# A decoder layer with a mixture of experts on one core: rows laid out by partition, expert biases moved, group tasks in halves

## The chip, the core and the metric

The kernel runs on one core of a Trainium2 chip. The metric is device time in microseconds (us) of one execution. A NeuronCore has TensorE (PE: matrix products into PSUM), VectorE (DVE), ScalarE (ACT), GpSimd (POOL) and SyncE (SP, which here only issues DMAs). Each runs its own list of instructions in order; they wait for each other on semaphores. PEld is PE's loading of weights.

## The reference, cut

```python
x = layernorm(x + attn(x, x, causal), ln1)              # 32 sequences of 128 tokens, D = 128
x = layernorm(x + attn(x, encoder, not causal), ln2)    # 16 heads of 8
# mixture of experts on the 4096 tokens
p = softmax(x @ rw + rb)                                # E = 8 experts
topw, topi = top_k(p, 2); topw = softmax(topw)
h = gelu(einsum('td,edf->etf', x, w1) + b1)             # FF = 512
eo = einsum('etf,efd->etd', h, w2) + b2
out = sum over the two chosen experts of topw * eo
x = layernorm(x + out, ln3)
```

All of it is float32. Only the two chosen experts of a token count.

## The kernel before, in words

**Units and halves.** A unit is one sequence of one attention: s (self, masked) or c (cross). Four sequences make a group (G = 4), so there are eight s groups and eight c groups. The units stand in one list: LEAD = 11 s units, then c and s in turn, then the c units that are left (lines 906 to 911). Each unit takes a slot of two halves. `half_slot(h)` (977) emits the work of one half: scores of the new unit and, with roles turned, of the unit two slots before (`both_scores`, 390), the row maximum on DVE (L425), exp on ACT (L433), for s a mask on POOL (L437); in even halves `values` (464) of the unit three slots before, in odd halves `outputs` (481). `ps_sc` and `ps_st`, where scores are put, have one buffer of PSUM each.

**Group tasks.** What is done once a group is put into a table of halves by hand (933 to 968), and `half_slot` runs what the table has for it. For an s group: `turn_input`, `keys`, `queries`, `values_of`, `residual`, later `turn_output`, `project` with `normalize` (304), `hand_over`. For a c group the same, and `keep_x2`, `route` (538), `place` (597) and `scatter` (678). Each task works on four sequences at once: a PSUM tile of 128x512, then one copy on ACT or one addition on DVE. `route` and `place` are generators of five steps, a step to a half. `scatter` issues two indirect DMAs on POOL to a half.

**The mixture.** `route` finds each token's two experts, `place` gives every (token, expert) pair a row in blocks of 128 rows of one expert, and `scatter` writes the token's row to DRAM (`xs`, 130 floats: the token, its row number, its first expert). There are two phases, PHASES: groups 0 to 5 and 6 to 7, with 55 and 23 blocks, 78 in all. When the last scatter of phase 0 has been issued, at half `start` (971), the blocks begin. `Pipeline.run` (851): for each block, SP fetches the weights of the block four ahead (`fetch_weights`, 745: 578 KB, w1, w2, b1 and a copy of b2 for every partition, into five buffers), PE does the first layer, ACT Gelu (L794), PE the second layer of the block before, DVE adds b2 from the weight tile (L810) into one of four `ot` buffers, POOL stores it by an indirect DMA to `eo` (L812). Every fourth block SP fetches 512 rows (`fetch_rows`, 733) and PE transposes them (`turn`, 759). After each block `beside` (1025) runs one more half of the table, and one step of each of up to two `combine`s (867). `combine` loads x2 and the two results of each token of a group (L872, L876), adds them with their weights, normalizes and stores (L901). The six groups of phase 0 begin theirs at the third block of phase 1, two at a time; the two of phase 1 after the last block.

**Queues.** SP issues all plain DMAs in the order of the program. A load that waits holds back everything after it on SP, weights too. The load of `gt` waits for all stores of its phase issued until then.

Of the kernel before, what the change touches and what calls it, by code (L numbers as in the profile page):

```python
# [24 lines left out]
PHASES = ((0, 6), (6, 2))  # L25
# [9 lines left out]
B2 = B1 + NFC  # L35
WP = B2 + P
# [5 lines left out]
LEAD = 11  # L42
# [19 lines left out]
def kernel(  # L62
# [140 lines left out]
    vs = [const.tile([P, G, H * VS + VC - VS - VW], F32, name=f"v_{i}") for i in range(3)]  # L203

    def blank(t):
        nc.gpsimd.memset(t, 0.0)
        nc.gpsimd.memset(
            t[:, :, : H * VS].rearrange("p b (h c) -> p b h c", c=VS)[:, :, :, HD:VW], 1.0
        )

    blank(vs[0])
# [41 lines left out]

    def load_router():
        nc.sync.dma_start(out=rw, in_=router_w)
        nc.sync.dma_start(
            out=rb, in_=router_b.rearrange("(o n) -> o n", o=1).broadcast_to([P, E])
        )
        nc.sync.dma_start(out=b1, in_=e_b1.rearrange("e (c f) -> (e c) f", f=P))

# [3 lines left out]
    blank_row = const.tile([P, XW], F32, name="blank_row")  # L264

    def routing_constants():
# [10 lines left out]

        i = setup.tile([P, B], I32, name="rowno_i")
        nc.gpsimd.iota(i, pattern=[[2 * P, B]], base=0, channel_multiplier=2)
        nc.vector.tensor_copy(rowno, i)  # L280
        later["free"] = counted([P, max(NBL)], [[2 * P, max(NBL)]], 0, "free")
        nc.gpsimd.memset(blank_row, 0.0)
        nc.gpsimd.memset(blank_row[:, TAG + 1 :], -1.0)
        nc.vector.tensor_copy(blank_row[:, TAG : TAG + 1], rowno[:, 0:1])
# [9 lines left out]
    x2d = tc.dram_tile([B, P, P], F32, name="x2d")  # L294
    xs = [tc.dram_tile([NBL[p] * P, XW], F32, name=f"xs_{p}") for p in range(NP)]
# [8 lines left out]
    def normalize(y, name):  # L304
# [3 lines left out]
        rs = small.tile([P, G], F32, tag="rs", name=f"rs_{name}")  # L308
        for t in range(G):
            nc.vector.bn_stats(st[:, t, :], y[:, t, :])  # L310
        for t in range(G):
            nc.vector.bn_aggr(mv[:, t, :], st[:, t, :])
        nc.gpsimd.tensor_scalar(rs, mv[:, :, 1], EPS, None, ALU.add)
        nc.gpsimd.tensor_tensor(rs, rs, mhalf, ALU.pow)
        yield
        for t in range(G):
            nc.vector.tensor_scalar(
                y[:, t, :], y[:, t, :], mv[:, t, 0:1], rs[:, t : t + 1], ALU.subtract, ALU.mult
            )

# [19 lines left out]
    def turned(src, name):  # L340
        pt = mm_tile([P, G, P], f"tp_{name}")
        for b in range(G):
            nc.tensor.transpose(pt[:, b, :], src[:, b, :], ident)
        return pt

    def turn_input(gr):
        pt = turned(gr.src, gr.name)
        gr.kvT = act.tile([P, G, P], F32, tag="kvT", name=f"kvT_{gr.name}", bufs=3)
        nc.scalar.copy(gr.kvT, pt)
        if gr.kind == "s":  # L350
            gr.qT = gr.kvT

    def keys(gr):
        pk = mm_tile([P, G, P], f"pk_{gr.name}")
        nc.tensor.matmul(pk, lhsT=gr.w.wk, rhs=gr.kvT, start=True, stop=True)
        gr.k = act.tile([P, G, P], F32, tag="k", name=f"k_{gr.name}", bufs=3)
        nc.scalar.activation(gr.k, pk, AF.Identity, bias=gr.w.bk)

    def queries(gr):

        pq = mm_tile([P, G, P], f"pq_{gr.name}")
        nc.tensor.matmul(pq, lhsT=gr.w.wq, rhs=gr.qT, start=True, stop=True)
        gr.qb = act.tile([P, G, 4, P], F32, tag="qb", name=f"qb_{gr.name}", bufs=3)
        for r in range(4):
            nc.scalar.activation(  # L365
                gr.qb[:, :, r, :], pq, AF.Identity,
                bias=gr.w.bqm[:, r : r + 1], scale=hmask[:, r : r + 1],
            )
# [4 lines left out]
    def values_of(gr):  # L373
        pv = mm_tile([P, G, P], f"pv_{gr.name}")
        for b in range(G):
            nc.tensor.matmul(pv[:, b, :], lhsT=gr.kvT[:, b, :], rhs=gr.w.wv, start=True, stop=True)
# [3 lines left out]
        nc.scalar.copy(  # L380
            gr.v[:, :, : H * VS].rearrange("p b (h c) -> p b h c", c=VS)[:, :, :, :HD],
            pv.rearrange("p b (h d) -> p b h d", d=HD),
        )
# [115 lines left out]
    def turn_output(gr):  # L499
        pt = turned(gr.o, f"o_{gr.name}")  # L500
        gr.oT = act.tile([P, G, P], F32, tag="oT", name=f"oT_{gr.name}")
        nc.scalar.copy(gr.oT, pt)

    def project(gr):

        py = mm_tile([P, G, P], f"py_{gr.name}")
        for b in range(G):
            nc.tensor.matmul(py[:, b, :], lhsT=gr.oT[:, b, :], rhs=gr.w.wo, start=True, stop=True)
        gr.y = act.tile([P, G, P], F32, tag="y", name=f"y_{gr.name}", bufs=3)
        nc.vector.tensor_tensor(gr.y, py, gr.resid, ALU.add)  # L510
        yield from normalize(gr.y, gr.name)

    def affineT(gr, i):

        pt = turned(gr.y, f"y_{gr.name}")
        t = act.tile([P, G, P], F32, tag=f"xT{i}", name=f"xT{i}_{gr.gi}")
        nc.scalar.activation(t, pt, AF.Identity, bias=lnbT[i], scale=lngT[i])
        return t

    def hand_over(gr, to):  # L520

        to.qT = affineT(gr, 0)
        to.resid = act.tile([P, G, P], F32, tag="x1", name=f"x1_{gr.gi}", bufs=4)
        nc.gpsimd.tensor_tensor(to.resid, gr.y, bc(lng[0], 1, G), ALU.mult)
        nc.gpsimd.tensor_tensor(to.resid, to.resid, bc(lnb1c, 1, G), ALU.add)

    def keep_x2(gr):
        gr.x2T = affineT(gr, 1)
        gr.x2 = act.tile([P, G, XW], F32, tag="x2", name=f"x2_{gr.gi}", bufs=3)
        x2 = gr.x2[:, :, :P]  # L530
        nc.gpsimd.tensor_tensor(x2, gr.y, bc(lng[1], 1, G), ALU.mult)
        nc.gpsimd.tensor_tensor(x2, x2, bc(lnb[1], 1, G), ALU.add)
        nc.gpsimd.tensor_copy(gr.x2[:, :, TAG], rowno[:, G * gr.gi : G * gr.gi + G])
        nc.sync.dma_start(
            out=x2d[G * gr.gi : G * gr.gi + G].rearrange("b p d -> p b d"), in_=x2
        )

    def route(gr):
# [25 lines left out]

        ex = small.tile([P, G], F32, tag="ex", name=f"ex_{gi}")
# [514 lines left out]
```

## Time and profile before

| | us |
|---|---|
| median of 3 runs (741.51 to 744.32) | 741.92 |
| the profiled execution, its time | 743.56 |
| its span, first to last instruction | 741.5 |
| PE busy, 8691 matmuls | 596.9 (80%) |
| PE weight loads | 486.4 (66%) |
| DVE busy | 421.4 (57%) |
| POOL busy | 364.7 (49%) |
| ACT busy | 347.8 (47%) |
| mean granted TensorE clock | 0.905 |
| moved by DMA | 88.06 MB |

Times in the profile are us unless marked ns. A row of the groups gives line, engine, operation, output and inputs, shapes and count, then busy time and the mean of one. The chain of work that ended last is followed back from the last instruction, at each step to what released it: here 43% PE, 17% DVE, 13% POOL, 13% DMA, 6% ACT. A row of the waits gives who waited for whom: total us, times, longest. Rows by stretch give the stretch, its length, and the busy us of each engine in it.

### The profile page before, as it was taken

What the parts mean: (1) busy time and instruction counts of PE and PEld (TensorE: products, weight loads), DVE (VectorE), ACT (ScalarE), POOL (GpSimd) and SP (SyncE); (2) the same over time, 40 slices, a digit from 0 to 9 for tenths busy, and PEclk for the clock granted to TensorE, in tenths of its full rate; (3) what the DMA queues carried; (4) which work ended last, traced back from release to release, by engine and by line L of the source; (5) the groups of instructions that cost most, each with busy time, mean ns of one, the idle gap of its engine ahead of it and who ended that gap; (6) DMA issues with size and microseconds to landing.
All of it is one profiled execution on the core that took longest, in us unless ns stands there. A gap on an engine that the chain in (4) does not pass through costs nothing.

```text
span 741.5 us, 21324 instructions
## 1 busy us (share of the span) xinstructions
PE 596.9 (80%) x8691; PEld 486.4 (66%) x8691; DVE 421.4 (57%) x1313; ACT 347.8 (47%) x671; POOL 364.7 (49%) x744
## 2 busy tenths in 40 slices
PE   5878898789898988888889878856887999875740
PEld 3556566667676766666667666746887999875630
DVE  2354665556776676687587587765522232274466
ACT  3335555465554556456455553533644555432310
POOL 2273555334447536645755633653776555433441
PEclk9798999999989999999999898976999999987975
DMA  6140603920100100100101100153998999979932
GB/s 135 26 98 3 152 22 78 187 35 4 44 2 27 49 2 24 52 2 17 45 3 31 31 2 10 38 179 113 314 309 283 354 355 344 331 252 307 280 122 89
DMA packets 73714, 88.06 MB, mean 119 GB/s; under 512 B 8080, under 2 KB 60336, under 8 KB 73616
## 3 DMA queue, kind: packets, MB, share of 16 engines
q1 hardware_dynamic: 68496, 77.19, 36.2%
q0 software_dynamic: 4544, 9.38, 3.5%
q8 instruction: 68, 1.11, 0.6%
q14 instruction: 30, 0.25, 0.1%
q10 hardware_dynamic: 576, 0.13, 0.1%
HBM read 67.90 MB, written 23.49 MB: 123 GB/s over the span
## 4 chain that ended last, share of the span: by engine, by line
PE 43%; DVE 17%; POOL 13%; DMA 13%; issue 6%; ACT 6%; SPq 1%; DVEq 0%; POOLq 0%
DMA wd<-wpk 7%; POOL xs L684 6%; PE st_s L410 5%; PE ph L789 5%; DVE m_c L425 5%; PE sc_s L397 4%; PE po L805 4%; PE po_s L472 4%; PE st_c L410 3%; DMA eo<-ot,to 3%; PE po_c L472 3%; ACT qb_s L365 3%; DVE m_s L425 2%; PE sc_s L417 2%; PE st_s L402 2%
## 5 line engine op out<-in xcount | busy, mean ns | idle before, releaser
L794 ACT ACTIVATE h<-ph,wd 128x128 f32<-128x128 f32 x312 | 88.8, 368 | 120.6 <-PE ph L789 84.1
L437 POOL TENSOR_SCALAR_AFFINE_SELECT pr_s<-pr_s 128x1024 f32<-128x1024 f32 x64 | 70.0, 1093 | 114.9 <-ACT pr_s L433 114.8
L789 PE MATMUL ph<-xT,wd 128*128 128x128 f32 x624 | 94.2, 298 | 39.6 <-DMA wd<-wpk 30.9
L812 POOL DMA_INDIRECT eo<-ot,to x78 | 77.1, 988 | 99.0 <-DVE ot L810 36.4
L425 DVE TENSOR_REDUCE m_s<-sc_s 128x8 f32<-128x1024 f32 x64 | 78.1, 1221 | 83.8 <-PE st_s L410 67.5
L789 PEld LDWEIGHTS ph<-xT,wd 128*128 128x128 f32 x624 | 83.2, 207 | 46.2 <-DMA wd<-wpk 33.4
L433 ACT ACTIVATE pr_s<-st_s 128x1024 f32<-128x1024 f32 x64 | 65.6, 1025 | 94.0 <-PE st_s L410 88.1
L425 DVE TENSOR_REDUCE m_c<-sc_c 128x8 f32<-128x1024 f32 x64 | 78.0, 1220 | 54.3 <-PE st_c L410 40.9
L433 ACT ACTIVATE pr_c<-st_c 128x1024 f32<-128x1024 f32 x64 | 65.5, 1024 | 63.2 <-PE st_c L410 59.4
L805 PE MATMUL po<-wd,h 128*128 128x128 f32 x624 | 89.1, 290 | 1.9 <-ACT h L794 1.9
L417 PE MATMUL sc_c<-k_c,qb_c 32*128 32x128 f32 x1024 | 78.4, 293 | 9.5 <-DVE m_s L425 5.0
L805 PEld LDWEIGHTS po<-wd,h 128*128 128x128 f32 x624 | 82.8, 206 | 2.1 <-ACT h L794 2.1
L417 PE MATMUL sc_s<-k_s,qb_s 32*128 32x128 f32 x1024 | 82.4, 303 | 0.2 <-ACT qb_s L365 0.2
L410 PE MATMUL st_c<-qb_c,k_c 32*128 32x128 f32 x1024 | 74.9, 282 | 0.0
L410 PEld LDWEIGHTS st_s<-qb_s,k_s 32*128 32x128 f32 x1024 | 73.1, 200 | 1.1 <-issue 1.1
L810 DVE TENSOR_TENSOR ot<-po,wd 128x128 f32<-128x128 f32 x78 | 22.3, 289 | 90.7 <-PE po L805 81.4
L417 PEld LDWEIGHTS sc_c<-k_c,qb_c 32*128 32x128 f32 x1024 | 65.7, 195 | 12.2 <-DVE m_c L425 6.3
L410 PE MATMUL st_s<-qb_s,k_s 32*128 32x128 f32 x1024 | 72.8, 283 | 0.9 <-issue 0.9
L410 PEld LDWEIGHTS st_c<-qb_c,k_c 32*128 32x128 f32 x1024 | 72.3, 195 | 0.5
L684 POOL DMA_INDIRECT xs<-x,slots x64 | 63.8, 997 | 15.7 <-issue 12.0
L417 PEld LDWEIGHTS sc_s<-k_s,qb_s 32*128 32x128 f32 x1024 | 68.8, 202 | 3.1 <-issue 2.1
L397 PE MATMUL sc_s<-causal,ident 128*128 128x512 bf16 x128 | 41.1, 405 | 24.7 <-DVE m_s L425 13.7
(226 smaller groups left out, 1070.4 us busy)
## 6 DMA issues: line engine op xcount, KB each, us to landing
wd<-wpk SPq DMA_DIRECT2D x78, 578.0 KB, 5.3
xt<-xs SPq DMA_DIRECT2D x18, 260.0 KB, 5.2
wpk<-in_L_xattn_e_w_dram SPq DMA_DIRECT2D x16, 256.0 KB, 6.9
gt<-eo SPq DMA_DIRECT2D x8, 512.0 KB, 6.3
xs<-blank_row SPq DMA_DIRECT2D x1, 3575.0 KB
xg<-in_x_dram SPq DMA_DIRECT2D x9, 256.0 KB, 3.3
eg<-in_ctx_dram SPq DMA_DIRECT2D x8, 256.0 KB, 3.5
x2d<-x SPq DMA_DIRECT2D x8, 256.0 KB, 2.5
```

The costliest lines, as they stand in the source:

```text
L397: nc.tensor.matmul(sc[:, i], lhsT=ident16, rhs=causal, start=True, stop=False)
L410: nc.tensor.matmul(st[:, i, r, :], lhsT=old.group.k[rowsof(g), old.b, :], rhs=old.group.qb[rowsof(g), old.b, r, :], start=False, stop=r == 3,)
L417: nc.tensor.matmul(sc[:, i, r, :], lhsT=new.group.qb[rowsof(g), new.b, r, :], rhs=new.group.k[rowsof(g), new.b, :], start=not new.masked, ...
L425: nc.vector.tensor_reduce(new.m[:, 8 * half : 8 * half + 8], sc.rearrange("p i r k -> p (i r) k"), AX.X, ALU.max,)
L433: nc.scalar.activation(old.pr[:, hs, :], st.rearrange("p i r k -> p (i r) k"), AF.Exp, scale=SCALE)
L437: nc.gpsimd.affine_select(out=old.pr[:, hs, :], in_=old.pr[:, hs, :], pattern=[[0, 8], [1, P]], compare_op=ALU.is_ge, fill=0.0, base=0, ch ...
L472: nc.tensor.matmul(po[VC * r : VC * r + VC, g, :], lhsT=u.group.v[:, u.b, at_v : at_v + VC], rhs=u.pr[:, h, :], start=e == 0, stop=e == 1,)
L684: i = nc.gpsimd.indirect_dma_start(out=xs[ph.p][:, :], out_offset=bass.IndirectOffsetOnAxis(ap=slots[:, k, t : t + 1], axis=0), in_=gr.x2[ ...
L789: nc.tensor.matmul(hid[:, c, :], lhsT=w[:, c * P : (c + 1) * P], rhs=self.xT[i // XB][:, i % XB, :], start=True, stop=True,)
L794: nc.scalar.activation(self.h[i][:, c, :], hid[:, c, :], AF.Gelu, bias=w[:, B1 + c : B1 + c + 1])
L805: nc.tensor.matmul(po, lhsT=h[:, c, :], rhs=w[:, W2 + c * P : W2 + (c + 1) * P], start=c == 0, stop=c == NFC - 1,)
L812: s = nc.gpsimd.indirect_dma_start(out=eo[p][:, :], out_offset=bass.IndirectOffsetOnAxis(ap=self.to[q][:, i % XB : i % XB + 1], axis=0), i ...
```

## The change

- `PHASES` becomes ((0, 5), (5, 3)): 47 and 31 blocks. `LEAD` becomes 12.
- DRAM by partition: `x2d` is [group, partition, sequence, 128], rows of `xs` that one partition reads lie together (four rows, 2080 bytes), and the two results of four tokens in `eo` too (4096 bytes). `place` computes the row numbers for it with integer steps; `rowno` follows.
- b2 leaves the weight tile (1028 floats a partition in place of 1156). `biases` multiplies the two chosen experts' weights into b2 by a matmul for a whole group, adds x2 and writes the sum to `x2d`, which `combine` starts from. The second layer's result is only copied to `ot`.
- `normalize` scales and shifts on ACT, with a bias of -mean * rs, in more steps. The weights of the two experts come from Tanh in place of Exp.
- Group tasks are done in two steps of two sequences; each step yields. `scatter` issues one DMA a step. Steps are put into halves by `book`, which takes, between two bounds, the half whose busiest engine would be least loaded by the planner's own costs.
- A group's `combine` begins as soon as its blocks are done (three blocks after the last that can hold its rows), not at the end of the phase; its `gt` takes a buffer of the tag "qb". Value tiles, `k` and `qb` have four buffers. The first fetch of rows is issued a half before the blocks, the first weights three.

The diff, cut to its core:

```diff
-PHASES = ((0, 6), (6, 2))
+PHASES = ((0, 5), (5, 3))
...
-B2 = B1 + NFC
-WP = B2 + P
+WP = B1 + NFC
...
-LEAD = 11
+LEAD = 12
...
@@ normalize
         for t in range(G):
-            nc.vector.tensor_scalar(
-                y[:, t, :], y[:, t, :], mv[:, t, 0:1], rs[:, t : t + 1], ALU.subtract, ALU.mult
-            )
+            nc.scalar.activation(
+                y[:, t, :], y[:, t, :], AF.Identity,
+                bias=rs[:, 1, t : t + 1], scale=rs[:, 0, t : t + 1],
+            )
+            if t == 1:
+                yield
...
+    PAIRS = (slice(0, 2), slice(2, 4))
...
     def keys(gr):
-        pk = mm_tile([P, G, P], f"pk_{gr.name}")
-        nc.tensor.matmul(pk, lhsT=gr.w.wk, rhs=gr.kvT, start=True, stop=True)
-        gr.k = act.tile([P, G, P], F32, tag="k", name=f"k_{gr.name}", bufs=3)
-        nc.scalar.activation(gr.k, pk, AF.Identity, bias=gr.w.bk)
+        gr.k = act.tile([P, G, P], F32, tag="k", name=f"k_{gr.name}", bufs=4)
+        for ab in PAIRS:
+            pk = pair(f"pk_{gr.name}", ab)
+            nc.tensor.matmul(pk, lhsT=gr.w.wk, rhs=gr.kvT[:, ab], start=True, stop=True)
+            nc.scalar.activation(gr.k[:, ab], pk, AF.Identity, bias=gr.w.bk)
+            yield
...
+    def biases(gr):
+        gi = gr.gi
+        w = small.tile([P, 2, G, E], F32, tag="comb", name=f"comb_{gi}", bufs=2)
+        for k in range(2):
+            nc.vector.tensor_tensor(
+                w[:, k], gr.onehot[:, k], bc(wts[:, k, G * gi : G * gi + G], 2, E), ALU.mult
+            )
+        nc.vector.tensor_tensor(w[:, 0], w[:, 0], w[:, 1], ALU.add)
+        yield
+        pw = mm_tile([G * E, P], f"pw_{gi}")
+        nc.tensor.transpose(pw, w[:, 0].rearrange("p b e -> p (b e)"), ident)
+        wT = small.tile([G * E, P], F32, tag="wT", name=f"wT_{gi}", bufs=2)
+        nc.scalar.copy(wT, pw)
+        yield
+        pb = mm_tile([P, G, P], f"pb_{gi}")
+        nc.tensor.matmul(pb, lhsT=wT, rhs=b2g, start=True, stop=True)
+        base = act.tile([P, G, P], F32, tag="base", name=f"base_{gi}", bufs=1)
+        nc.vector.tensor_tensor(base, pb, gr.x2[:, :, :P], ALU.add)
+        nc.sync.dma_start(out=x2d[gi], in_=base)
...
-        nc.scalar.activation(ex, ex, AF.Exp)
+        nc.scalar.activation(ex, ex, AF.Tanh, scale=0.5)
...
@@ second_layer
-            nc.vector.tensor_tensor(ot, po, w[:, B2:], ALU.add)
+            nc.vector.tensor_copy(ot, po)
...
+    def book(lo, hi, cost, *call):
+        def then(h):
+            old = busy.get(h, (0.0,) * 4)
+            return max(a + b for a, b in zip(old, cost) if b)
+        h = min(range(lo, max(lo, hi) + 1), key=lambda h: (then(h), h))
+        busy[h] = tuple(a + b for a, b in zip(busy.get(h, (0.0,) * 4), cost))
+        return at(h, *call)
+    def chain(lo, hi, *parts):
...
+        for n, (cost, call) in enumerate(todo):
+            left = len(todo) - 1 - n
+            end = book(lo, hi - left, cost, *call)
+            lo = end if hi - end + 1 >= left else end - 1
+            ends.append(end)
...
+        h, far = max(h, sent), 1 + (gi == NG - 1)
+        for b in range(G):
+            for k in range(2):
+                at(h, scatter, c, ph, b, k)
+                h += far
+        sent = h
+        if gi == PHASES[0][1] - 1:
+            ready = h
...
+    start = max(behind, ready)
+    at(start - 3, blocks.prepare)
+    at(start - 1, blocks.first_rows)
...
+        summed = {}
+        for p, (g0, n) in enumerate(PHASES):
+            for g in range(n):
+                i = NS + 2 * G * (g + 1) - 1 + 3
+                key = (p, i) if i < NBL[p] or p == NP - 1 else (p + 1, i - NBL[p])
+                summed[key] = groups["c", g0 + g]
```

## The prediction, as put on record

> **What bounds the kernel now.** I read the slices of the span first, then the busy time by stretches, then the chain and the waits.
>
> ```profile
> PE   5878898789898988888889878856887999875740
> ...
> PEclk9798999999989999999999898976999999987975
> DMA  6140603920100100100101100153998999979932
> ```
>
> Tenths of busy time, 18.5 us a slice. Attention fills slices 1 to 26 with PE at 0.8 to 0.9 and idle DMA. Then PE falls to 0.5 (the handover), the MoE blocks follow with PE and DMA both near 1.0, then both fall, and at the end PE is at 0.
>
> ```profile
> 317.00:375.00 58.00, 50.99 (x921) 38.69 (x920) 40.99 (x117) 31.40 (x44) 32.43 (x65) 0.94 0.07 20
> ...
> 480.00:507.00 27.00, 12.92 (x162) 10.76 (x160) 18.00 (x92) 6.63 (x10) 14.43 (x28) 0.71 0.45 148
> 507.00:540.00 33.00, 30.08 (x233) 29.18 (x232) 17.62 (x90) 20.25 (x57) 20.42 (x36) 0.87 0.74 244
> ...
> 580.00:640.00 60.00, 56.44 (x493) 55.12 (x493) 15.80 (x64) 33.13 (x116) 30.55 (x59) 1.00 1.01 349
> 640.00:690.00 50.00, 35.57 (x253) 34.31 (x253) 27.50 (x118) 16.91 (x60) 20.64 (x36) 0.83 0.90 283
> 690.00:715.00 25.00, 16.96 (x106) 16.15 (x105) 14.26 (x58) 7.04 (x25) 10.48 (x18) 0.80 0.64 204
> 715.00:742.00 27.00, 0.01 (x1) 0.00 (x0) 13.16 (x49) 0.00 (x0) 4.71 (x7) 0.60 0.36 105
> ```
>
> Stretch, length, then busy us of PE, PEld, DVE, ACT, POOL, then clock, DMA share, GB/s. A block is 17 PE instructions (8 + 8 + 1 transpose), so 580 to 640 holds 29 blocks at 2.07 us with PE at 94%: the good rate. 507 to 580 holds 29.5 at 2.5 us. 640 to 715, where six groups are combined, holds 21 at 3.6 us. The last 27 us have no PE work.
>
> Inside attention the reduce L425 shows the beat: where little stands beside it, starts are 2.49 us apart with a new cross unit (464.93, 467.42, 469.90 in DVE's timeline) and 3.19 us with a new self unit. Each score tile has one buffer, so scores wait for the reduce (1.22 us) before them. A steady period of 16 halves (8 units) took 58.4 us against 8 x 2.49 + 8 x 3.19 = 45.4 us of beat. PE is busy 51.3 us of it, so 7.1 us are all that better placing could return there.
>
> ```profile
> SPq L754 <- DVE ot L810: 35.5, 29, 3.2
> ```
>
> SP's own waits: 29 weight fetches waited for the DVE add that reads the bias out of the weight tile.
>
> **Part 1: attention.** A c and an s group bring some 15 us of PE work a period (rows L343, L355, L362, L376, L508, L545 divided by 8 groups), nearly all of the 13 us above the beat. Cutting it in twos removes none of it. It can fill halves in which PE waits: of those I count in one period a half of 5.5 us where POOL is busy 5.0 us (two scatters of 2 x 1.27 us, a mask, the rsqrt), one of 3.2 us with 1.5 us of PE behind DVE's normalize, and several of 0.5 to 1 us behind place, route and queries. One scatter to a half (0.99 + 0.09 + 0.2 us to issue) and booking remove most; I take idle 7.1 -> 3.
>
> Added: the bias step on PE, a transpose (0.2) and a 512-wide matmul (nearest row L362, 1.1): +1.3 us a period. On DVE three small steps (0.18 each) and an add of 512 (L510, 0.68), five integer steps in place (about 0.9). Normalize's 4 x 0.38 to 0.46 us move from DVE to ACT (nearest row: Gelu 128x128 with a bias pointer, 0.37 us). ACT also pays a fixed part for each extra half copy (586 ns for 512 wide, 372 for 256: 0.16 each, some 22 a period, 3.5 us). ACT goes from 31 to about 38 us of 58 and stays under PE. So a period changes by -4.1 + 1.3 = -2.8; 5.25 periods give **-15**. I worked the booking through on paper: where the window is shorter than the chain, the first parts collapse into one half (nine parts of s0 in half 15, of s7 in half 111, four parts of each c group). There PE waits for ACT's copy and DVE for POOL's rsqrt (1.04 us); I set these, some 6 us, against what the last 22 halves (78 us, beat 55) gain. The fourth value tile adds 1.3 us of POOL memsets (1.07 + 0.22) to half 9, which is 8.1 us long already for the routing constants; it is in those 6 us. The wider clearing of rows and the dropped bias copies cost and win nothing: DMA is 10% busy there (share 0.07 in the row above). Bounds: +8 (nothing recovered, all additions paid) and -30 (idle of the period to 0).
>
> A rule speaks against the move. The Trainium skill, "ScalarE: Activation LUTs", Rules for kernel authors, sends mul and add to VectorE. By its fixed costs a 128-wide ACTIVATE with two pointer operands is about 0.39 us back to back (an estimate); here DVE's own step took 0.36 to 0.46 us, so rule and row agree that nothing is won per instruction and only the busier engine matters.
>
> Exp becomes Tanh. The trace has six table loads of 1283 ns: one at the start, then none until the last group's two Exps and three for Gelu around them. If Tanh needed its own, 6 groups x 2 x 1.28 = 15 us of ACT would come into attention, mostly beside PE. That is the upper bound; 0 is the lower. I take 0 there, and 5 us of ACT in the first blocks (two groups now route there), hidden behind POOL. The same page, Table sets, lists Tanh with Exp in one set, which would make it 0 in attention; no run here shows it.
>
> **Part 2: handover.** With five groups in phase 0, its last scatter is booked at half 133, and the blocks start at 134 (before: 137). Now, from the last reduce to the first block:
>
> ```profile
> 476.06 1.23 DVE L425 TENSOR_REDUCE m_c<-sc_c 128x8 f32<-128x1024 f32 x1 [0.31 <-PE st_c L410]
> ...
> 499.72 1.08 PE L766 MATMUL px<-ident,xt 128*128 128x128 f32 x4 [4.34 <-DMA xt<-xs]
> ...
> 506.21 1.01 PE L789 MATMUL ph<-xT,wd 128*128 128x128 f32 x3 [5.40 <-DVE xT L781]
> ```
>
> That is 506.2 - 477.3 = 28.9 us. After: six halves of mostly POOL work (1.27 scatter, about 0.65 of other tasks each) 11.5, landing 2.7, rows 2.8 (both in the chain at 493.9 and 496.8), transposes 0.6, copy 0.7: 18.3. **-10**; bounds -17 (all but the DMAs hidden) and -2 (place of group 5 delays the copy on DVE as place of group 6 does now).
>
> **Part 3: the blocks.** Packets, from the trace's DMA records (medians): 512 B 27 ns, 1024 B 46, 2048 B 84, 4624 B 179, so about 8.4 ns + 0.037 ns a byte. Weights go from 4624 to 4112 B (160 ns; 128 x 19 / 16 = 0.15 us a block), rows xt from 4 x 28 to 85 ns (0.05 us a block), gt and x2d save 0.4 us a group. In all 78 x 0.2 + 3 = 19 us of the 191 us of DMA time from 507 to the end. And a weight buffer is freed by PE, not by DVE's add. A good block then is PE's 1.95 to 2.0 us.
>
> Against it: POOL. In blocks 0 to 18 it issues 19 stores of results and 16 scatters (groups 5, 6) at 1.27 us, plus 6.7 us of rsqrt and x2: 51 us, and only four ot buffers let PE run ahead. I take 48 us. Blocks 19 to 77: 59 x 2.0 = 118. Combines: the bursts of 640 to 715 cost 21 x (3.57 - 2.07) = 31 us for six groups, 5.3 each. Seven now come one by one, every eight blocks, with 1 MB each, but each gt load still waits on SP for the newest result to land (5.2 us median), with the next weights queued behind it. Between 1.3 (only the bytes) and 5.3 I take 4: 28. Sum 194 against 715 - 507 = 208: **-14**. Bounds -35 and +10.
>
> **Part 4: the end.** Two groups in step become one: stores landed, gt load, 8 x 0.35 of sums, statistics, rsqrt, 4 x 0.37 on ACT, two passes of 0.69, a store of 2.3 us: about 20.5 with the hand-offs, against 26.5. **-6**, bounds -9 and -2.
>
> **Sum.** 743.6 (the profiled execution; span 741.5) - 15 - 10 - 14 - 6 = 698.6. That execution lay 1.6 above the median of 741.9, so 697 against the runs; I say **698**.
>
> **Rivals.** A: everything overlaps. Attention -25, handover -14, blocks -32 (0 to 18 at 2.3 us, 1.5 a combine), end -7: 666. For it: the good rate of 580 to 640. Against: POOL's count above. B: placing gains nothing, PE sets every half and the bias step is paid: attention +5, rest as above: 718. For it: 51.3 of 58.4 us are already PE's. Against: the halves behind POOL. C, slower: SP's queue. The gt load's wait holds the weights, so blocks 19 to 77 run at the 3.36 us of 640 to 690: 59 x 1.36 = 80 in place of 28, +52: 750. It decides above about 11 us a combine (then 745). For it: that stretch itself. Against: there four groups came in 15 blocks, and pairs waited for the store of the pair before.
>
> **Chances.** Forecast (680 to 712) 0.56, A 0.18, B 0.16, C 0.10. The range reaches to A's and B's times and the bounds beside them: 668 to 734. A measurement here tells about 0.5% (3.7 us) from no change; of C's 0.10 a part ends near nothing: faster 0.87, same 0.04, slower 0.09.
>
> **What would show it.** Attention: last L425 reduce near 460 (before 476), PE share above 0.9 in the middle. Handover: 18 us from it to the first ph. Blocks: no "SPq L754 <- DVE ot", waits on POOL in the first 19, weights waiting behind gt at each combine. End: 20 us without PE. Table loads before the last scores would prove the Tanh step wrong; a middle period of 58 us or more Part 1; blocks over 2.6 us after the 19th Part 3.

## The result: no change that counts

The changed kernel took 741.48 us (median of 20 runs, 736.7 to 745.9), the kernel before 744.54 in the same series: ratio 0.9976, 95% interval 0.9952 to 1.0000. The forecast was 698. The profiled execution took 742.25 us, its span is 740.5, its mean granted clock 0.897 (before 0.905). PE is busy 606.3 us, DVE 413.0, ACT 404.6 (before 347.8), POOL 366.9; DMA moved 82.48 MB (before 88.06).

The slices of the span, to be laid beside those of the prediction:

```profile
PE   5696899999988999899889789868996786689750
...
PEclk9578999999999899899899999757999988899985
DMA  5010342630000100010110010052896788799852
```

Attention's PE row is a little fuller from slice 6 to 19. The start has a clock of 5 in the second slice, the handover (slices 26 to 28) one of 7, 5, 7, and the blocks no longer hold DMA at 9: it falls to 6 and 7 at regular places.

The trace gives the boundaries of the four terms of the prediction. "First block" is the start of the first ph.

| | before | after | forecast of the change | found |
|---|---|---|---|---|
| first reduce | 13.2 | 16.6 | | |
| start of the 23rd half's reduce | 100.1 | 109.1 | | |
| last reduce | 476.1 | 467.8 | -15 | -8.3 |
| its end to the first block | 28.9 | 31.3 | -10 | +2.4 |
| first block to PE's end | 208.8 | 214.0 | -14 | +5.2 |
| of it blocks 0 to 18 | 49.5 | 53.7 | | |
| PE's end to the end | 26.5 | 26.2 | -6 | -0.3 |

So three of four terms brought nothing or less, and the first, which went the right way, lost 9 us at its start. By stretch, in the columns of the prediction (a middle period; the handover; blocks 0 to 18, 19 to 46, 47 to 76; the end):

```profile
291.10:349.10 58.00, 51.87 (x939) 39.97 (x935) 42.51 (x121) 36.82 (x72) 32.72 (x67) 0.94 0.06 20
468.90:500.30 31.40, 22.08 (x200) 16.00 (x200) 11.13 (x66) 9.71 (x18) 12.66 (x28) 0.60 0.35 125
500.30:554.00 53.70, 48.08 (x373) 45.24 (x374) 33.85 (x174) 30.90 (x95) 34.85 (x62) 0.92 0.67 221
554.00:641.90 87.90, 61.60 (x480) 58.29 (x478) 35.29 (x152) 36.66 (x126) 48.29 (x90) 0.89 0.80 271
641.90:711.50 69.60, 62.54 (x507) 61.89 (x508) 27.20 (x113) 38.10 (x131) 34.88 (x64) 0.92 0.88 306
714.30:740.50 26.20, 0.05 (x1) 0.00 (x0) 10.11 (x41) 3.29 (x8) 7.69 (x13) 0.56 0.28 84
```

The fourth row is the surprise: 28 blocks, 3.14 us each, PE idle for 26 of 88 us. Most intervals between blocks there are 1.8 to 2.9 us (4.4 after block 19). After blocks 22, 30, 38 and 46 (counted from 0) they are 5.8, 8.8, 8.6 and 8.7, with 3.2 to 3.6 for the next. Each lies four blocks behind the one at which a combine issues its loads (18, 26, 34, 42). In the second row PE has work for 22 of 31 us, at a clock of 0.60 (before 14.8 us at 0.75).

**One combine, in the timeline** (start, length, engine, line; in brackets the idle time before and what ended it):

```profile
628.25 0.58 SPq L940 DMA_DIRECT2D acc<-x2d  x1
...
634.62 0.32 SPq L942 DMA_DIRECT2D gt<-eo  x1
...
635.04 0.38 SPq L816 DMA_DIRECT2D wd<-wpk  x1
...
638.11 1.14 DVE L955 SCALAR_TENSOR_TENSOR acc<-gt,wts,acc 128x128 f32<-128x128 f32 x4 [6.52 <-DMA gt<-eo]
...
638.79 1.03 POOL L878 DMA_INDIRECT eo<-ot,to  x1 [9.79 <-DVE acc L955]
...
641.16 0.68 DVE L847 COPY xT<-px 128x512 f32<-128x512 f32 x1
...
641.94 2.04 PE L855 MATMUL ph<-xT,wd 128*128 128x128 f32 x8 [6.22 <-DVE xT L847]
```

SP stands 6 us at gt, until the newest store of a result has landed, with the weights behind it (635.04). The stores after it wait on POOL, 9.79 us, because they write into the tensor that gt reads. DVE waits in order for gt, with the copy of the next four blocks' rows (L847) behind it. PE runs dry, and its next block runs at half clock (2.04 for eight matmuls; 1.06 before).

**The waits**, those of the whole span that bear on this (total us, times, longest):

```profile
POOL eo L878 <- DVE acc L955: 48.4, 11, 9.8
DVE acc L955 <- DMA gt<-eo: 46.0, 8, 7.4
...
PE ph L855 <- DMA wd<-wpk: 21.6, 8, 6.4
PE ph L855 <- DVE xT L847: 12.5, 5, 6.2
...
PE py_c L542 <- ACT oT_c L533: 9.7, 8, 2.2
```

and SP's own:

```profile
SPq L942 <- DMA eo<-ot,to: 44.5, 15, 6.5
SPq L820 <- PE po L871: 38.3, 35, 4.1
```

The second of SP's rows is as forecast: a weight buffer is freed by PE, no longer by DVE's add. The first is the new wait.

### The profile page after: what moved, and what is told of

Read it like the earlier page. It is cut to its first block, busy times and chain, and to the rows that moved or that the text cites. A ratio compares the mean times of both kernels' runs of the same rounds, so it can differ in the third digit from the quotient of the medians.

```text
span 740.5 us, 21783 instructions
## 1 busy us (share of the span) xinstructions
PE 606.3 (82%) x8779; PEld 499.5 (67%) x8779; DVE 413.0 (56%) x1321; ACT 404.6 (55%) x919; POOL 366.9 (50%) x747
## 2 busy tenths in 40 slices
DMA packets 48038, 82.48 MB, mean 111 GB/s; under 512 B 7968, under 2 KB 26464, under 8 KB 47936
## 5 line engine op out<-in xcount | busy, mean ns | idle before, releaser
L855 PE MATMUL ph<-xT,wd 128*128 128x128 f32 x624 | 92.2, 295 | 34.1 <-DMA wd<-wpk 21.6
L464 ACT ACTIVATE pr_s<-st_s 128x1024 f32<-128x1024 f32 x64 | 65.8, 1029 | 79.0 <-PE st_s L441 78.7
L448 PE MATMUL sc_c<-k_c,qb_c 32*128 32x128 f32 x1024 | 79.1, 295 | 10.7 <-DVE m_s L456 9.0
L448 PE MATMUL sc_s<-k_s,qb_s 32*128 32x128 f32 x1024 | 80.7, 300 | 0.0
L441 PE MATMUL st_c<-qb_c,k_c 32*128 32x128 f32 x1024 | 76.8, 290 | 0.0
L441 PEld LDWEIGHTS st_c<-qb_c,k_c 32*128 32x128 f32 x1024 | 75.8, 205 | 0.7
L876 DVE COPY ot<-po 128x128 f32<-128x128 f32 x78 | 22.5, 288 | 59.6 <-PE po L871 48.9
```

The lines of the kernel that those rows point to most:

```text
L441: nc.tensor.matmul(st[:, i, r, :], lhsT=old.group.k[rowsof(g), old.b, :], rhs=old.group.qb[rowsof(g), old.b, r, :], start=False, stop=r == 3,)
L448: nc.tensor.matmul(sc[:, i, r, :], lhsT=new.group.qb[rowsof(g), new.b, r, :], rhs=new.group.k[rowsof(g), new.b, :], start=not new.masked, ...
L464: nc.scalar.activation(old.pr[:, hs, :], st.rearrange("p i r k -> p (i r) k"), AF.Exp, scale=SCALE)
L855: nc.tensor.matmul(hid[:, c, :], lhsT=w[:, c * P : (c + 1) * P], rhs=self.xT[i // XB][:, i % XB, :], start=True, stop=True,)
L876: nc.vector.tensor_copy(ot, po)
```

## Experiments

Theory after this look: the early combine costs 8 us a time through its waits; the handover runs at half clock and its rows stand behind weights; attention loses at its start, where the planner folds many parts into one half, and where DVE waits for POOL. Rivals: the combine's work and bytes themselves, ACT's new load, the bias step on PE.

The kernel before took 746 us beside the first four runs and 772 to 777 beside the others, on other chips, so a ratio is always to the kernel before on the same chip. Ratios from different chips can't be compared closely: the same code has 0.959 on one and 0.944 on another (e2_own6, e13_both below). Stage times of blocks are compared within one chip. The changed kernel itself ran only in the series of the result, where the kernel before took 744.5; it is set beside the first four runs alone.

### Combine after the phase, as before (e1_late)

```
-            gr = summed.pop((ph.p, i), None)
-            if gr:
-                sums.append(combine(gr))
+            if ph.p and i == 2:
+                g0, n = PHASES[ph.p - 1]
+                sums.extend(combine(groups["c", gi]) for gi in range(g0, g0 + n))
...
-        sums.extend(combine(gr) for _, gr in sorted(summed.items()))
+        g0, n = PHASES[-1]
+        sums.extend(combine(groups["c", gi]) for gi in range(g0, g0 + n))
```

> The changed kernel with the old timing of the combines: phase 0's five groups from the third block of phase 1 on, two at a time, phase 1's three groups after the last block. Theory (what was lost in the blocks is the early combine: SP waits for the newest store, the stores wait for gt, DVE waits for gt): the blocks 19 to 46 run at 2.0 to 2.1 us each, 57 us in place of the 86 of the changed kernel; five combines at 5 to 6 us each come back in the blocks after the 50th (some 27 us), two stalls of phase 1 go (-9) and the end grows by a third group (+9). Whole time 715 to 735, and no gap over 4 us before the 47th block. Rival (the blocks are slow for another reason, POOL's stores or ACT's load): blocks 19 to 46 stay at 80 to 88 us, whole time 740 to 755.

738.25 us, ratio 0.9899 (0.9854 to 0.9944). The blocks 19 to 46:

```profile
554.70:615.70 61.00, 56.26 (x481) 53.78 (x479) 20.07 (x86) 32.25 (x114) 45.16 (x86) 1.00 0.96 331
```

61.0 us against 87.9, PE at 92%, clock 1.00: the gaps belong to the combine, not to POOL's stores or ACT, which are nearly as busy as before (45 and 32 us, 48 and 37). With e3_weights below, on the same chip and with its combines as in the changed kernel, these blocks took 82.4 us. Most of the gain is given back, and the whole is slower than the 715 to 735 expected: blocks 47 to 76 take 78.7 us (69.6), and three groups' combines after the last block make the end 38.8 (26.2).

### Combine freed of its waits (e2_own, e2_own6)

```
-        for j in phases[p].done:
+        n = NS + 2 * G * (gr.gi - PHASES[p][0] + 1)
+        for j in phases[p].done[:n]:
             tc.add_manual_dep(i.ins, j.ins.name, SYNC, reason="results")
+        for j in phases[p].done[n:]:
+            tc.declare_no_dep(i.ins, j.ins, reason="rows of later groups")
...
+            for j in self.ph.loads:
+                tc.declare_no_dep(s.ins, j.ins, reason="rows of earlier groups")
```

A group's rows can lie only in the first n blocks of its phase; the last two lines are the later stores' side. In e2_own6 the combine also begins three blocks later:

```
-                i = NS + 2 * G * (g + 1) - 1 + 3
+                i = NS + 2 * G * (g + 1) - 1 + 6
```

> The changed kernel, but the gt load of a group waits only for the stores of the blocks that can hold its rows, and the stores of later blocks no longer wait for that load. Same place of the combine in the code. Theory: the store wait on SP shrinks from 6 us to 2 or 3 (the youngest store it needs is two blocks older) and POOL's wait of 10 us for gt goes; DVE may still wait for gt some 2 to 4 us. A combine costs 3 to 4 us in place of 8: 78 blocks and combines 15 to 25 us shorter, the end 4 to 6 us shorter because group 7 no longer stands behind group 6. Whole time 712 to 725. Rival (the work and bytes of the combine themselves cost the 8 us): no change, 736 to 744.

> As the run before it, with the combine begun three blocks later, so that the youngest store that gt needs has landed when SP comes to it. Theory: SP does not wait at all at gt; gaps between blocks at the combines under 3 us; what is left is the DVE's wait for gt's own landing (6.4 us, with two blocks of 2 us between the load and the first sum), 1 to 3 us each. Whole time 703 to 718. Rival (work and bytes): 736 to 744; rival (only the wait on SP matters and the stores' wait does not): the same as the run before it.

725.94 us, 0.9717 (0.9676 to 0.9758), and 714.57 us, 0.9594 (0.9545 to 0.9644). The first lies just above its range, the second inside, though intervals of 4.0 to 4.5 us after three blocks are left where under 3 were expected. In the second, blocks 19 to 46 and 47 to 76:

```profile
551.90:621.10 69.20, 58.96 (x480) 55.82 (x478) 33.08 (x143) 36.35 (x126) 49.65 (x91) 0.98 0.96 331
621.10:684.20 63.10, 58.00 (x508) 57.01 (x508) 28.31 (x120) 37.23 (x129) 35.01 (x65) 1.00 0.99 357
```

From the first block to PE's end 186.4 us (214.0), and the end takes 21.0 (26.2). PE's matmuls in these stretches are the same as in the changed kernel (480 and 508 records, there 480 and 507), and so, within 1%, are the bytes moved (rate times length, 45 MB): what went is waits, and with them half clock.

### Which of the two waits (e13_place, e13_stores, e13_load, e13_both)

Four kernels on one chip, all with the later place: with both waits; without the stores' wait for gt; without gt's wait for newer stores; without both.

> The changed kernel with each combine begun three blocks later and nothing else: the gt load still waits for the newest store, the later stores still wait for the load. Theory (the newest store is always about 5 us from landing, however late the combine begins): the gaps of 8 us stay, whole time within 4 us of the changed kernel's 741 in proportion to the kernel before on this chip. Rival (the place alone does it): 22 to 30 us shorter.

> As e13_place, and later stores no longer wait for the gt load; the load still waits for the newest store. Theory A (SP's wait, with the weights behind it, makes the gap): the gaps stay at 7 to 9 us, within 5 us of e13_place. Theory B (the stores' wait on POOL makes it: results pile up in four buffers and PE stops): the gaps fall under 4 us, 15 to 25 us shorter than e13_place.

> As e13_place, and the gt load waits only for the stores of the blocks that can hold its rows; later stores still wait for the load. Theory A: as e13_both, 20 to 30 us shorter than e13_place, though POOL still waits 6 us for each load. Theory B: gaps of 5 to 7 us stay, at most 10 us shorter than e13_place.

> Both waits gone at the later place (the same code as e2_own6, beside the three others on their chip): 24 to 32 us shorter than e13_place, gaps at the combines under 4.5 us. Under theory A or B alone it equals one of the two runs before it within 4 us; if each wait alone suffices to make the gap, both of those stay near e13_place and only this one gains.

| | median us | ratio, interval | blocks 19 to 76 | the end |
|---|---|---|---|---|
| both waits | 763.76 | 0.9781 (0.9676 to 0.9886) | 165.5 | 25.7 |
| stores free | 755.08 | 0.9734 (0.9667 to 0.9800) | 155.6 | 22.7 |
| gt free | 742.67 | 0.9578 (0.9499 to 0.9658) | 150.9 | 20.5 |
| both free | 734.03 | 0.9436 (0.9347 to 0.9525) | 138.3 | 19.9 |

Neither theory alone. In the blocks gt's wait on SP is worth 14.5 us, the stores' wait on POOL 9.9, both 27.2: they nearly add up. The place alone removes neither: with both waits the intervals behind the six combines are 4.5, 7.4, 8.1, 6.9, 4.5 and 6.8 us, only three blocks later than before, and SP still waits for the newest store, 33.1 us in all (2.6 in e13_both). By the medians e13_place was 11 us faster than the changed kernel's 0.998 lets expect on this chip (774.8), where at most 4 were expected. As the changed kernel did not run on it, whether the later place has a part in that stays open.

### Early combine in the kernel before (e4_early)

```
-            if ph.p and i == 2:
-                g0, n = PHASES[ph.p - 1]
-                sums.extend(combine(groups["c", gi]) for gi in range(g0, g0 + n))
+            gr = summed.pop((ph.p, i), None)
+            if gr:
+                sums.append(combine(gr))
```

> The kernel before with one part of the change alone: each group's combine eight blocks after the other, in its own phase, instead of in a burst after it. Nothing else changed (weights of 4624 B with their biases, attention as before). Theory (an early combine costs 8 us through SP's wait for the newest store, the stores' wait for gt and DVE's wait; the burst cost about 5 a group): six to seven gaps of 7 to 10 us between blocks appear from the 19th block on, the burst at the blocks 61 to 76 goes; blocks 12 to 22 us longer in sum, the end 3 to 8 us shorter: 746 to 765 against 742 to 746 for the kernel before, in the same proportion on a slower chip. Rival (the early combines are harmless, the loss comes from other parts of the change): 725 to 740, as forecast for this term.

781.93 us against 774.30, 1.0096 (1.0036 to 1.0157): this part alone makes the kernel about 1% slower. Behind the combines, after blocks 22, 30, 38, 46, 54 and 62, the intervals are 6.5, 5.4, 4.7, 4.3, 6.8 and 5.0 us. The size per combine stays open: its attention on this chip lasted to 496.6 (476.1 in the profile of before) with nothing of it changed. The end did not shrink as expected (25.2 us, before 26.5). The changed attention ended at 468 to 473 us in the series of the result and on the chips of e2_own6 and e13. So a ratio from a chip on which the kernel before takes 772 to 777 us may hold a gain that the series of the result did not have; why the old attention is slower there is not known.

### Weights ahead in the handover (e3_weights)

```
-    at(start - 3, blocks.prepare)
+    at(start - 12, blocks.prepare)
```

> The changed kernel with the first four weight fetches issued nine halves earlier, so that the rows of the first block are not behind them on SP and in the DMA queues, nor they behind the store of the base. Theory (rows landed 6.5 us after their issue because 2 MB of weights stood ahead of them; 2.8 us before): the rows land 3 to 4 us sooner, from the last reduce to the first block 31 -> 27.5 us, the whole time 3 to 4 us shorter, 737 to 739. Rival (the rows are late for the scatters' own sake, the weights only look it): no change in that stretch. The last halves themselves may lose up to 1 us to the earlier traffic.

741.54 us (six runs, 731.73 to 744.03), 0.9878 (0.9824 to 0.9933). Set beside the kernel before, this is better than the changed kernel by some 7 us going by the ratios and by 2 going by the medians, where 3 to 4 were expected: the size stays open. The handover did shrink, from the last reduce's start to the first block 27.0 us against 32.7 in e1_late on the same chip. In the profiled execution (743.93, one of the two longest) the first ten blocks gave it back: 37.5 us, 20.5 of them at half clock, against 32.2 with 8.8. Whether the shorter runs lost it too is not shown.

### DVE's add beside POOL (e5_sums)

In three halves of attention DVE's last add of `place` lasts 2.9 us where it takes 0.2 otherwise. The timeline of one of them, in the changed kernel:

```profile
350.56 1.05 DVE L734 TENSOR_TENSOR which<-end,d_at 128x312 f32<-128x312 f32 x1
...
351.48 1.13 POOL L751 DMA_INDIRECT xs<-x,slots  x1 [0.17 <-issue]
351.64 0.48 DVE L736 TENSOR_REDUCE part<-which 128x39 f32<-128x312 f32 x1
352.16 2.86 DVE L737 TENSOR_TENSOR sums<-sums,part 128x39 f32<-128x39 f32 x1
...
352.64 1.28 POOL L564 TENSOR_TENSOR x<-x,lnb1c 128x512 f32<-128x512 f32 x1
...
353.86 1.10 POOL L468 TENSOR_SCALAR_AFFINE_SELECT pr_s<-pr_s 128x1024 f32<-128x1024 f32 x1
...
356.98 0.58 PE L448 MATMUL sc_c<-k_c,qb_c 32*128 32x128 f32 x2 [2.95 <-DVE m_s L456]
```

The add, which reads two operands from SBUF, ends when POOL's select after L564 is done; the reduce with one operand (L736) beside the same scatter takes its 0.48. PE waits 2.95 us for the scores' reduce behind it and then runs at half clock for 6.8 us (355.6 to 362.4 in the trace's clock records). The Trainium skill, "GPSIMD Engine Reference", Specifications, says that GpSimd's SBUF interfaces are shared with VectorE and contended by DVE instructions with two SBUF inputs: the rows agree.

```
-        nc.vector.tensor_tensor(ph.sums, ph.sums, part, ALU.add)
+        nc.gpsimd.tensor_tensor(ph.sums, ph.sums, part, ALU.add)
```

This run and the three after it have the freed combine at the later place, as e2_own6, and ran on one chip.

> The changed kernel with the freed combine (own stores only, three blocks later) and one instruction moved: the last add of place (L737, 128x39, two operands in SBUF), which took 2.86 us instead of 0.2 in three halves of attention because POOL was at a scatter and an add then, goes from DVE to POOL. Theory (these halves hold up the reduce, PE idles 2.7 us, and a stretch of half clock of 6.8 us follows each: 244, 299, 357): each of the three periods gets 4 to 6 us shorter, the last reduce moves from 469 to 452 to 458, and the three stretches of half clock go. Whole time 697 to 704. Rival (the next DVE instruction takes over the wait for POOL, or PE is bound by its own work): the last reduce stays within 2 us of 469, whole time 708 to 716.

723.95 us, 0.9355 (0.9299 to 0.9412). The two middle periods of 16 halves went to 55.8 and 55.7 us, where the other runs on this chip have 56.1 to 59.0 (58.1 and 58.0 in the changed kernel): what the prediction had (55.6). The expected 11 to 17 us did not come, only 2 to 5 from the 47th half to the last: another step with two operands, the weighting in `biases`, takes over the wait.

```profile
L582 DVE TENSOR_TENSOR comb<-onehot,wts 128x32 f32<-128x32 f32 x8 | 6.2, 809 | 0.0
```

It has a mean of 809 ns here, 191 in e2_own6: its first step takes 1.8 to 1.9 us in the same three groups. On this chip the add that was moved lasted 1.8 to 1.9 us in the three other runs, so the wait went from one instruction to the next at about its size. The rival was half right, and how much of the shorter periods is this edit's doing is not certain, as two of the other runs have one of 56.1 and 56.2 without it.

### The start (e6_start)

```
-            h0 - 13, h0 - 2,
+            h0 - 13 if gi != 1 else 0, h0 - 2,
```

> The changed kernel with the freed combine, and the second self group's turn, keys and queries booked from half 0 on and not ahead of the first scores. Theory (they delay the first reduce by 3.4 us and the half clock of the start lasts longer for it): the first reduce comes at about 15 us in place of 18, half 22 some 2 to 5 us earlier, and that stays to the end: 705 to 712. Rival (PE has to do this work anyway before half 8, and the first 22 halves are bound by loads and POOL's constants): half 22 and the end within 1 us, 708 to 716.

721.09 us, 0.9340 (0.9293 to 0.9387). First reduce 12.2 (18.0 to 19.6 in the three others on this chip), the 23rd half's 100.6 (108.2 to 111.9), the last reduce 461.0 (465.5 to 469.2). More than expected, and it stays: booking the second group ahead of the first scores costs some 5 to 8 us.

### ACT's load and the bias step (e7_norm, e8_nobias)

The first puts normalize's four steps back on DVE. The second leaves the second layer's biases out of the output:

```
-        nc.sync.dma_start(out=x2d[gi], in_=base)
+        nc.sync.dma_start(out=x2d[gr.gi], in_=gr.x2[:, :, :P])
```

> The changed kernel with the freed combine, and normalize's four steps back on DVE (subtract and multiply), in the same halves. Theory (neither engine is the bound there; ACT's load is no cause of the lost gain): attention within 2 us, whole time 707 to 718. Rival (ACT at 405 us of 740, in order ahead of the exps, delays the scores): the last reduce 4 to 8 us earlier, whole time 700 to 706. Third possibility: DVE waits for POOL's port in these steps as before the change (1.11 us in place of 0.34 once a group), attention 3 to 6 us longer.

> The changed kernel with the freed combine, without the bias step: the store to x2d takes x2 itself, so the second layer's biases are left out of the output. It measures what the step costs. Prediction's term: 1.3 us of PE a period, some 7 us of attention, and the 2.07 us of its matmul in the handover at half clock. Theory: attention 5 to 8 us shorter, handover 1 to 2 us, first blocks 2 to 4 us (a PE wait of 2 us for DVE's weighting in front of each of the later groups' transposes goes). Whole time 697 to 705. Rival (the step fits into idle PE time): attention within 2 us, whole time 705 to 712.

730.91 us, 0.9445 (0.9391 to 0.9498), and 721.17 us, 0.9317 (0.9254 to 0.9380). From the 47th half to the last reduce the four runs of this chip took 282.4 (e5), 287.1 (e6), 284.7 (e7) and 285.2 (e8): neither ACT's load nor the bias step is felt there (284.4 to 286.6 in the changed kernel and the seven runs before e5 that have its attention). Both rivals fall for attention. But without the bias step the handover is 27.6 us from the last reduce's start, with it 33.6 to 34.2. SP's queue in e6_start and, in the last row, e8_nobias:

```profile
483.29 0.34 SPq L596 DMA_DIRECT2D x2d<-base  x1
483.68 2.99 SPq L816 DMA_DIRECT2D wd<-wpk  x4
487.00 0.92 SPq L803 DMA_DIRECT2D xt<-xs  x2
...
486.79 0.80 SPq L788 DMA_DIRECT2D xt<-xs  x2
```

In e6_start the rows are issued 5.4 us after the last scatter (481.6), behind the base's store and four weights; in e8_nobias 1.5 us after it (485.3), the weights long before (438.8). So about 4 of the 6 us are the wait of that store in SP's queue, and not PE's time for the step's matmul.

### The fold and the handover (e10_cap, e9_hand, e11_all)

All with the freed combine and e6's start. e10_cap limits what `chain` folds into one half:

```
+        cap, there = -(-len(todo) // (hi - lo + 1)), 0
...
+            there = there + 1 if ends and ends[-1] == end else 1
-            lo = end if hi - end + 1 >= left else end - 1
+            lo = end if hi - end + 1 >= left or there >= cap else end - 1
```

e9_hand issues the scatters of phase 0's last group two to a half, so that the blocks start at half 132, and books that group's bias step after the end of attention:

```
-                h += far
+                h += k if gi == PHASES[0][1] - 1 else far
...
+        late = behind + 3 if gi == PHASES[0][1] - 1 else h
-        chain(h, h + 5, (lambda c=c: biases(c), ...
+        chain(late, late + 5, (lambda c=c: biases(c), ...
```

> As e6_start, with the planner's fold limited: where a chain has more parts than halves (13 in 10 for each cross group, 13 in 5 for the first self group), each half takes two (three) of them and not the first half all that are over. Theory (four parts in one half make PE wait 1.9 to 2.2 us for ACT's copies, once for each cross group, with half clock behind it; 9.7 us of waits at L542 in all): the last reduce 5 to 9 us earlier than e6_start's 461, and the half clock from 471 on comes later or not at all, handover 3 to 8 us shorter. Rival (the parts put elsewhere hold up other halves as much): the last reduce within 2 us, handover within 2 us.

> The changed kernel with the freed combine and the later start of the second self group (as e6_start), and in the handover: the scatters of phase 0's last group two to a half, so that the blocks start at half 132, and that group's bias step three halves after the attention's end, so that neither its matmul at half clock nor its store stands ahead of the first block's weights and rows. Theory (the handover is slow because six halves run at half clock, 3.8 us each against 1.9 assumed, and because the rows stand behind the base's store and 2 MB of weights): from the last reduce to the first block 33 -> 20 to 24 us; the first ten blocks give back up to 5. Whole time 6 to 11 us under e6_start's on the same chip. Rival (PE at half clock does the same work whatever the order, and scatters and rows are hidden behind it): 30 to 33 us, no gain.

> Both edits of the two runs before it together. If both theories hold: attention 453 to 457, handover 17 to 22, blocks as in those runs, whole time 10 to 18 us under e6_start's. If only the handover's holds: as e9_hand.

| | median us | ratio, interval | last reduce | its start to the first block |
|---|---|---|---|---|
| e6_start, other chip | 721.09 | 0.9340 (0.9293 to 0.9387) | 461.0 | 33.6 |
| e10_cap | 693.29 | 0.8972 (0.8921 to 0.9023) | 442.5 | 27.6 |
| e9_hand | 709.26 | 0.9162 (0.9121 to 0.9204) | 461.1 | 21.6 |
| e11_all | 690.16 | 0.8912 (0.8872 to 0.8951) | 448.2 | 18.5 |

The fold was worth 18.6 us of attention, twice the most that was expected (e9_hand, on the same chip as e10_cap, has 461.1 too): 5.2 before the 23rd half, 2.7 in the middle, 10.7 in the last 21 halves (half 112 took 6.4 us and now 4.1, 113 5.1 and 3.0, 120 7.1 and 3.1). PE's wait for ACT's copy between the folded parts, 9.7 us in all above, left PE's waits in e10_cap but for that of the self groups:

```profile
PE py_s L542 <- ACT oT_s L533: 1.0, 2, 0.6
```

The part on the clock held: half clock came at 450.7, 8.3 us after the last reduce's start (3.0 in e6_start), and the handover shrank by 6 us. With both edits, in e11_all, the rows are no longer behind weights:

```profile
461.97 0.80 SPq L803 DMA_DIRECT2D xt<-xs  x2
...
464.80 1.08 PE L832 MATMUL px<-ident,xt 128*128 128x128 f32 x4 [3.77 <-DMA xt<-xs]
...
466.67 2.08 PE L855 MATMUL ph<-xT,wd 128*128 128x128 f32 x8 [0.78 <-DVE xT L847]
```

2.8 us from the issue to the transposes. In attention 5.7 us of e10's gain are missing in e11. Of these 2.8 are there by the 23rd half, before the handover's edit can act, in the half-to-half times of the start, which differ from run to run. e11_all is 0.891 of the kernel before on its chip (e10_cap 0.897; the intervals overlap): the change's idea with its waits mended.

## Why the prediction was wrong, step by step

**Attention, -15, found -8.3.** "I take idle 7.1 -> 3" failed: a middle period took 58.0 us, PE 51.87 busy, 6.1 idle. The planner counts each engine's own time and does not know that DVE waits for POOL; with one such add moved the period is 55.7, the forecast 55.6, though e6 and e8 each have a period of some 56.1 without that. "I set these, some 6 us, against what the last 22 halves gain" was the mis-sized term: the folds cost 18.6 us (e10_cap). The start is missing from the working: 5 to 8 us (e6_start). With both mended the last reduce comes at 442.5, 33.6 us earlier than in the profile of before, which is of another chip, and 54 us earlier than the old attention had on e10's own chip (e4_early): more than rival A's 25 either way. Right were: normalize on ACT neither gains nor costs in attention, and Tanh needs no table load (there is none between 1.25 and 493.70 us). The 1.3 us a period for the bias step were not felt (e8_nobias).

**Handover, -10, found +2.4.** "six halves of mostly POOL work ... 11.5" took 18.6 (from the reduce's end, 469.0, to the last scatter's, 487.6): PE, not POOL, set these halves, at half clock from 471.6 to 492.1. "rows 2.8" took 6.6. The rows of it, from the timeline of the changed kernel:

```profile
470.61 1.17 PE L542 MATMUL py_c<-woc,oT_c 128*128 128x128 f32 x8 [1.90 <-ACT oT_c L533]
...
489.28 0.34 SPq L596 DMA_DIRECT2D x2d<-base  x1
489.67 1.88 SPq L816 DMA_DIRECT2D wd<-wpk  x4
491.87 0.98 SPq L803 DMA_DIRECT2D xt<-xs  x2
...
498.44 1.09 PE L832 MATMUL px<-ident,xt 128*128 128x128 f32 x4 [6.20 <-DMA xt<-xs]
```

PE pauses 1.9 us at a folded half, and half clock begins. The base's store waits for DVE's add, the weights stand behind it in SP's order, and the rows are fetched behind 2 MB. The working has the landing and the rows, but not this store, which shares SP's queue with both. From the reduce's end, e9_hand and e11_all need 20.4 and 17.3 us; the forecast was 18.3.

**Blocks, -14, found +5.2.** "Blocks 19 to 77: 59 x 2.0" nearly holds between combines (e1_late: 2.18 a block with none). "Between 1.3 (only the bytes) and 5.3 I take 4" failed: the interval of 2 us grew by 4 to 7, the next by 1.5, and the four combines of blocks 19 to 46 cost 27 us against e1_late, 6.8 each. Rival C named the mechanism, SP's queue with the weights behind gt, but had its price as a rate and said nothing of the other half: the stores that wait for the load, and DVE's order. (Its 11 us a combine would make 698 + 7 x 7 = 747, not 745.) e13 splits the two waits, 14.5 and 9.9 us. Without them the stage takes 186.4 us, where the forecast had 194. The packets were as forecast (4112 B 160 ns, 2080 B 85). For blocks 0 to 18 the forecast of 48 us met 53.7: PE waits 2.2 us for a copy on ACT, which stands behind a table load and an Exp that waits for DVE, and 2.1 for DVE's chain of the groups still in attention's tail.

**End, -6, found -0.3.** "Two groups in step become one" did not happen: group 6's gt waited until 712.2, POOL's stores for it until 716.9, so group 7's gt was issued at 724.3. Freed, the end takes 21.0 us; the forecast was 20.5.

Rival B (718) was wrong in its reason, since the bias step cost nothing that could be felt in attention. That the total came near the old time is chance: the losses (the start, the folds, the handover's store, the two waits of the combine) happen to cancel the gains.

## What to carry to other kernels

A load that is moved ahead of its phase's end must wait only for the writes it needs, and later writes must not wait for it: otherwise it stops the queue it stands in, and the engine that writes. A planner that fills quiet halves needs a rule for what doesn't fit and for engines that hold each other up; folding the rest into one half cost 18.6 us, more than the 8.3 that attention won in the end. Follow each moved store and load past everything that its queue issues next, at the stage where the queue has no slack.

## What the runs showed of the hardware

- **The clock.** In the handover the granted clock stayed at 0.50 for 20.5 us, though PE was busy throughout part of it:

```profile
480.00:490.00 10.00, 10.00 (x104) 6.98 (x100) 2.65 (x18) 3.39 (x6) 6.13 (x15) 0.50 0.09 28
```

  The trace's clock records hold only 1.0 and 0.5, in stretches of multiples of 3.4 us. The Trainium skill, "TensorE: Matmul & The Clock Gate", Part 1: The HAM clock gate, says the same of the window, and that one busy window brings full clock back. Here four such windows between 471.6 and 488.7, in which the profile has PE busy throughout, did not; many of those matmuls are 32 rows high, and whether that is the reason was not tried.
- **Tables.** A Tanh after Gelu needed no table load (in the changed kernel: a load for Gelu at 513.11, Tanh at 520.60, the next load at 532.33 for Exp).
- **Chips.** The same code took 714.6 us on one chip and 734.0 on another (e2_own6, e13_both), and most of it lies from the handover on. In their profiled executions (709.9 and 737.1 us): last reduce 469.3 and 472.8, blocks 0 to 18 51.2 and 65.1, 19 to 76 132.3 and 138.3 us.
